# A GATv2 layer on Trainium2: groups of 8 rows with 64 places instead of 32 rows with 16, and one head's relu on ScalarE

## The chip, the cores and the metric

The kernel runs as one program on one core of one Trainium2 chip. The metric is the device time of one execution in microseconds (us). A profiled execution of the same program gives the trace that all views below come from; its span runs from the first to the last instruction of the core. PE is TensorE (PEld its weight loads), DVE is VectorE, ACT is ScalarE, POOL is GpSimd, SP is SyncE.

## What is computed

Two graph layers on 3327 nodes with 128 features, the node count padded to 3328 = 26 blocks of 128. Only layer 0 (four attention heads over a dense adjacency matrix that is about 2% filled) is touched by the change in more than names. Per head:

```python
x1 = x @ w1                       # one row per destination node i
x2 = x @ w2                       # one row per source node j
E = leaky_relu(x1[:, None, :] + x2[None, :, :], 0.01)
s = E @ a
s = exp(tanh(s / 8.0) * 8.0) * A_shape
s = s / sum(s, axis=-1)
out = leaky_relu(s @ x @ Wlin.T, 0.01)
```

The heads are concatenated, multiplied by `w` and added to `x`. Layer 1 is a normalised graph convolution with the same adjacency matrix.

Since leaky_relu(v) = 0.01 v + 0.99 relu(v), the score of an edge (i, j) is 0.01 a.x1_i + 0.01 a.x2_j + 0.99 a.relu(x1_i + x2_j). The kernel also uses relu(x1 + x2) = max(x2, -x1) + x1: with the maximum instead of the relu, the term of x1 outside has to be a.x1 in place of 0.01 a.x1. Both forms occur below.

## The kernel before, in words

All of the work is in `_sparse_layers`. A block is 128 destination rows. Only the filled entries of a row are worked on: each row gets 64 places (32 for each half of the columns), found by DVE with repeated MAX8 and MATCH_REPLACE8 (L422 to L456); entries beyond these are an overflow of two further tiles. A table in DRAM holds, for each node j, a row of adjacency values, features, a term of x2 and the four heads' x2.

**Gathers.** A block is two halves (`hb`) of 64 rows, a half is four windows (`w` 0 to 3) and one overflow window (`w` 4). For a window POOL issues 8 indirect DMAs (L597, tile `g`), one for each tile of 128 edges; for the overflow it issues 2 (tile `ge`). That is 68 a block. There are four `g` buffers. A buffer is free again when the last user of its window, the aggregation (L702), is done; `fetch` then lets the next window's gathers be issued.

**Stage z** (`stage_z`, groups `m` 0 to 8, two to a window; 18 groups a block). A group before the change is 32 rows x 16 places = 4 tiles of 128 edges. For each pair of heads (`hp`) PE turns the gathered x2 of 2 heads x 4 tiles into a PSUM tile `z` of two banks (L624, 8 transposes) and DVE makes `r = max(z, -x1)` of 128x1024 in one instruction (L640). Group 8, the overflow, adds x1 on PE (L629) and takes the maximum of a small part on DVE (L635) and a relu of the rest on ACT (L637).

**Stage r** (`stage_r`) of the group before: PE contracts `r` with `a` for four heads (L653), each head's result in its own 32 rows of the PSUM tile `s`.

**`finish`**, a generator that goes on by one step at each `slot()`, works a window off: ACT copies `s` to `ssb` (L662), DVE makes `wq` (L666), PE turns the scores (L671), DVE adds the terms of x2 and x1 (L674, L677), ACT does tanh and exp (L682, L684), DVE makes the weights `wt` (L693), and PE aggregates (L702): 8 matmuls of 32 output columns, each with an output at partitions 32*cg to 32*cg + 31 and in half `u` of the PSUM tile `ag`. Before the change tile t has cg = t % 4 and u = t // 4, so each window uses all four cg.

**Order.** It is written out by hand, and each engine does its instructions in that order. The main loop emits for group i: a slot, stage z of i (with four slots inside), stage r of i - 1, a slot. A slot advances the finishing generators, a share of the preparation of the next block (`prep`: the adjacency turned by PE and copied by ACT at L365 and L367 with a DMA from ACT's queue at L370, DVE's search for entries, a sum over the whole adjacency rows on ACT at L443, x1 at L553 to L570) and the gathers. Most instructions are emitted some slots before their result is needed.

**Names that the change touches:** `x1n` is -x1 with features on partitions (L561), `pex` the term of x1 outside the relu for each edge (L563 to L570, from `p_all`, whose first four columns are a.x1 and last four 0.01 a.x1), `idx` the row numbers for the gathers, `k.oi` and `x1b` the overflow's selectors.

The line that fixes the PSUM tiles of stage z, two bufs of two banks, is this, used once for heads 0 and 1 and once for heads 2 and 3:

```python
z = ps_z.tile([P, 2, BANK], F32, name="z")
```

Of the kernel before, what the change touches and what calls it, by code (L numbers as in the profile page):

```python
# [9 lines left out]
F32 = mybir.dt.float32  # L10
AF = mybir.ActivationFunctionType
OP = mybir.AluOpType
# [219 lines left out]
def _sparse_layers(tc, nc, x, adj, w1, w2, a, wlin, w, gw, gb, gb_sb, gwT, x_sb, dinv, flag, ident, out):  # L232
# [24 lines left out]
    with ExitStack() as l0:  # L257
# [29 lines left out]
        ph = l0.enter_context(tc.tile_pool(name="ph", bufs=2))  # L287
        pr = l0.enter_context(tc.tile_pool(name="pr", bufs=2))
        pv = l0.enter_context(tc.tile_pool(name="pv", bufs=1))
        pe_ = l0.enter_context(tc.tile_pool(name="pe", bufs=1))  # L290
        ps_tr = l0.enter_context(tc.tile_pool(name="ps_tr", bufs=2, space=PSUM))
        ps_z = l0.enter_context(tc.tile_pool(name="ps_z", bufs=2, space=PSUM))
        ps_s = l0.enter_context(tc.tile_pool(name="ps_s", bufs=1, space=PSUM))
        ps_a = l0.enter_context(tc.tile_pool(name="ps_a", bufs=1, space=PSUM))
        ones = pv.tile([P, D], F32, name="xn")
        nc.vector.memset(ones, 1.0)
# [56 lines left out]
        def prep(b, k):  # L353
# [204 lines left out]
            for h in range(H):  # L558
                nc.tensor.matmul(pm[:, h * P:(h + 1) * P], w1_sb[:, h, :], hTb, start=True, stop=True)
            x1n = pb.tile([P, H, P], F32, name="x1n")  # L560
            nc.scalar.activation(x1n, pm[:, :H * P].rearrange("p (h i) -> p h i", h=H), AF.Copy, scale=-1.0)  # L561
            pmx = pb.tile([P, 16, H], F32, name="pmx")
            nc.vector.tensor_tensor(pmx, tmask[:, :, None].to_broadcast([P, 16, H]),  # L563
                                    p_all[:, b, None, :H].to_broadcast([P, 16, H]), OP.mult)
            yield
# [4 lines left out]
            nc.scalar.copy(pex, pm[:, :16 * H].rearrange("p (t h) -> p t h", h=H))  # L570
            k.x1b, k.x1n, k.pex = x1b, x1n, pex
            yield
# [5 lines left out]
        def gather(b, hb, w):  # L578

            k = blks[b]  # L580
            tab = tables[b % 2].rearrange("(r u) -> r u", u=1)
            if w == NW:
                if b + hb == 0:
                    state["over"] = pe_.tile([P, OVT, WIDE], F32, name="ge")
                    nc.vector.memset(state["over"][HALF:, FOUND:], 0.0)
                g, n, at = state["over"], FOUND, k.idxo[:, hb]
                rows = b * P + HALF * hb
                c0, n0 = (0, FEAT + COLS) if hb == 0 else (FEAT, BODY + FEAT)
                nc.sync.dma_start(g[:HALF, FOUND, :n0], tables[b % 2][:NP * ROW].rearrange("(r c) -> r c", c=ROW)[rows:rows + HALF, c0:c0 + n0])
            else:  # L590
                g, n, at = rows_in(), WT, k.idx[:, w, WT * hb:WT * hb + WT]

            def one(t):
                lo, hi = (0, FEAT + COLS) if hb == 0 else (0, BODY + FEAT)
                if w < NW:
                    lo, hi = (8 * t, hi) if hb == 0 else (0, BODY + 8 * t + 8)
                return nc.gpsimd.indirect_dma_start(out=g[:, t, lo:hi], out_offset=None, in_=tab,  # L597
                                                    in_offset=bass.IndirectOffsetOnAxis(ap=at[:, t:t + 1], axis=0))

            queue.extend((k, hb, w, partial(one, t)) for t in range(n))  # L600
            k.g[hb, w] = g
# [10 lines left out]
        def stage_z(k, hb, m, slot):  # L612
            n = 4 * P if m < 8 else FOUND * P
            arrived(k, hb, m // 2)
            g = k.g[hb, m // 2]
            out = []
            for hp in range(2):
                z = ps_z.tile([P, 2, BANK], F32, name="z")
                r = pr.tile([P, 2, BANK], F32, name=f"r{hp}")
                for i in range(2):  # L620
                    h = 2 * hp + i
                    c0 = k.f0[hb] + PROJ + h * D
                    for q in range(n // P):
                        nc.tensor.matmul(z[:, i, q * P:(q + 1) * P], g[:, m % 2 * 4 + q, c0:c0 + D], ident,  # L624
                                         is_transpose=True, start=(q == 0 or m < 8), stop=(m < 8), skip_group_check=True)
                    if m == 8:
                        nc.tensor.matmul(z[:, i, n:n + HALF], g[:HALF, FOUND, c0:c0 + D], ident[:HALF, :HALF],
                                         is_transpose=True, start=False, stop=False, skip_group_check=True)
                        nc.tensor.matmul(z[:, i, :n], k.x1b[:, h * D:(h + 1) * D], k.oi[:, hb * n:(hb + 1) * n],  # L629
                                         start=False, stop=True, skip_group_check=True)  # L630
                    if i == 0:
                        slot()
                slot()
                if m == 8:
                    nc.vector.tensor_tensor(r[:, :, n:n + HALF], z[:, :, n:n + HALF],  # L635
                                            k.x1n[:, 2 * hp:2 * hp + 2, HALF * hb:HALF * hb + HALF], OP.max)
                    nc.scalar.activation(r[:, :, :n], z[:, :, :n], AF.Relu)  # L637
                else:
                    r0 = HALF * hb + 32 * (m % 2)
                    nc.vector.tensor_tensor(r.rearrange("p h (i s) -> p h i s", s=16), z.rearrange("p h (i s) -> p h i s", s=16),  # L640
                                            k.x1n[:, 2 * hp:2 * hp + 2, r0:r0 + 32, None].to_broadcast([P, 2, 32, 16]), OP.max)
                out.append(r)
            return out

        def stage_r(k, hb, m, rs):
            n = 4 * P if m < 8 else FOUND * P + HALF
            at = m % 2
            if state["scores"] is None:
                state["scores"] = ps_s.tile([P, BANK], F32, name="s")
                nc.vector.memset(state["scores"], 0.0)  # L650
            k.s = state["scores"]
            for h in range(H):
                nc.tensor.matmul(k.s[32 * h:32 * h + 2, :n], sel[:, h, 31 - at:33 - at], rs[h // 2][:, h % 2, :n],  # L653
                                 start=(at == 0), stop=(at == 1 or m == 8))


        def finish(k, hb, w):
# [3 lines left out]
            ssb = ph.tile([P, BANK], F32, name="ssb", bufs=1)  # L661
            nc.scalar.copy(ssb[:, :nk * P], s[:, :nk * P])  # L662
            if w < NW:
                wq = pb.tile([P, WT, 8], F32, name="wq")
                diag = bass.AP(g.tensor, g.offset + BODY * hb, [list(g.ap[0]), [WIDE + 8, 8], [1, 8]])
                nc.vector.tensor_tensor(wq, diag, qmask[:, None, :].to_broadcast([P, WT, 8]), OP.mult)  # L666
            yield
            yield
            pt = ps_tr.tile([P, 4, P], F32, name="tr")
            for q in range(nk):  # L670
# [5 lines left out]
                                    g[:, :, f0 + D:f0 + D + H].rearrange("p (m k) h -> p m k h", m=nm), OP.add)  # L676
            nc.vector.tensor_add(sc[:, :nt], sc[:, :nt], k.pex[:, 8 * hb:8 * hb + 8] if w < NW else  # L677
                                 k.ex[:, OVT * hb:OVT * hb + OVT, 42:42 + H])
            yield
# [11 lines left out]
            if w < NW:  # L691
# [7 lines left out]
                yield  # L699
                for t in range(WT):  # L700
                    u, cg = t // 4, t % 4
                    nc.tensor.matmul(ag[32 * cg:32 * cg + 32, u, :WORK], wt[:, t].rearrange("p h q -> p (h q)"),  # L702
                                     g[:, t, f0:f0 + WORK], start=(w == 0 and t < 4), stop=False, skip_group_check=True)
                allow("g")
# [229 lines left out]
        def strip_in(s):  # L934

            n = min(4, NB - 4 * s)
            r0 = pr.tile([P, 2, BANK], F32, name="r0").rearrange("p k (b d) -> p k b d", b=4)[:, :, :n]
            r1 = pr.tile([P, 2, BANK], F32, name="r1").rearrange("p k (b d) -> p k b d", b=4)[:, :, :n]
            rows = slice(4 * s * P, (4 * s + n) * P)
            nc.sync.dma_start(r0[:, 0], xn_d[rows, :].rearrange("(b p) d -> p b d", p=P))  # L940
            if finished(4 * s):
                nc.sync.dma_start(r1[:, 0], part1_d[:, rows].rearrange("p (b i) -> p b i", b=n))
            if s in early:
                nc.sync.dma_start(r0[:, 1], part2_d[:, rows].rearrange("p (b i) -> p b i", b=n))
            return n, rows, r0, r1

        def strip_out(s, po, n, rows, r0, r1):

            ot, t, xo = r0[:, 1], r1[:, 1], r0[:, 0]
            po = po[:, :n * P].rearrange("p (b i) -> p b i", b=n)  # L950
# [23 lines left out]
        def layer1():  # L974
            ending, sums, ins = [], {}, {}
            for i, (s, j) in enumerate(work):
# [3 lines left out]
                if s not in sums:  # L980
                    sums[s] = ps_z.tile([P, 2, BANK], F32, name="z")[:, 0]
                if j == min(NB - 1, first_column(s) + 4 * (s not in front)):
# [202 lines left out]


        pgs = [l0.enter_context(tc.tile_pool(name=f"pg{i}", bufs=1)) for i in range(4)]

# [167 lines left out]
```

## Time and profile before

| What | Value |
|---|---|
| Time before, median of 12 runs | 2525.42 us (2522.43 to 2528.16) |
| The profiled execution's own time | 2529.1 us |
| Its span | 2527.4 us |
| Granted TensorE clock | 0.98 |
| Instructions | 52430 |
| HBM read and written | 754.47 MB, 113.22 MB |

The page gives a group of instructions as its line, its engine and operation, its operands, a count, the busy time and the mean duration, and behind the second bar the idle time of its engine just before, with what ended it. A timeline line is start, duration, engine, line, operands, count and, in brackets, the idle time before and its releaser. A matmul with four-byte operands is recorded twice unless it is a transpose. The stages that the page shows in 40 slices are: 0 to about 65 us of loading and table building, then the 26 blocks to about 2400 us, then the rest of layer 1. In the blocks the slices hardly differ from each other.

### The profile page before, as it was taken

How to read it: one execution, taken by the hardware profiler on the slowest of the kernel's cores; microseconds unless marked ns; L12 is line 12 of the kernel's file. 1: busy time of each engine (PE TensorE's matmuls, PEld its weight loads, DVE VectorE, ACT ScalarE, POOL GpSimd, SP SyncE). 2: the span in 40 equal slices, each digit the busy share in tenths (PEclk: the TensorE clock that was granted, in tenths of full speed). 3: DMA queues.
4: the chain of work that ended last, by engine and by line, in shares of the span. 5: the costliest groups of instructions: out<-in, count | busy, mean ns of one | idle time of the engine just before them, and what ended most of it. 6: DMA issues, size and time to landing. Idle time of an engine off the chain costs nothing.

```text
span 2527.4 us, 52430 instructions
## 1 busy us (share of the span) xinstructions
PE 2286.5 (90%) x19410; PEld 1579.1 (62%) x19410; DVE 2092.3 (83%) x6478; ACT 687.3 (27%) x1703; POOL 1735.9 (69%) x1822
## 2 busy tenths in 40 slices
PE   6589899989999998999999999999999999999977
PEld 4456666666666666666666666666666666666643
DVE  7688988898898888889889888988988898896623
ACT  4122232223223222322222232222232223222110
POOL 3567777777777776777777777777777777777700
PEclk9799999999999999999999999999999999999999
DMA  9999999999999999999999999999999999999995
GB/s 306 382 321 320 355 330 317 349 347 322 327 356 330 313 346 329 290 337 359 320 323 353 340 315 339 355 318 320 343 339 316 337 349 306 330 325 350 348 273 155
DMA packets 417844, 826.94 MB, mean 327 GB/s; under 512 B 38435, under 2 KB 288815, under 8 KB 414255
## 3 DMA queue, kind: packets, MB, share of 16 engines
q0 software_dynamic: 141440, 619.41, 70.1%
q1 hardware_dynamic: 165343, 147.87, 18.4%
q10 hardware_dynamic: 110800, 56.25, 7.7%
q8 instruction: 156, 2.56, 0.4%
q14 instruction: 105, 0.86, 0.1%
HBM read 754.47 MB, written 113.22 MB: 343 GB/s over the span
## 4 chain that ended last, share of the span: by engine, by line
PE 35%; DVE 28%; DMA 18%; POOL 10%; issue 7%; ACT 0%; SPq 0%; DVEq 0%; ACTq 0%; POOLq 0%
DMA g<-table,idx 14%; DVE r L640 13%; PE z L624 10%; POOL g L597 10%; PE s L653 6%; PE z L629 3%; DVE cand L422 3%; PE ag L702 2%; PE tr L671 2%; DVE cand L456 2%; DVE codes L410 2%; DVE lists L453 2%; DMA g<-AT_d 2%; PE z L985 1%; PE tr L921 1%
## 5 line engine op out<-in xcount | busy, mean ns | idle before, releaser
L597 POOL DMA_INDIRECT g<-table,idx x1664 | 1613.0, 969 | 612.9 <-issue 415.8
L624 PE MATMUL z<-ident,g 128*128 128x128 f32 x6656 | 919.8, 279 | 134.0 <-DVE r L640 115.2
L640 DVE TENSOR_TENSOR r<-z,x1n 128x1024 f32<-128x1024 f32 x832 | 1010.2, 1216 | 35.8 <-PE z L624 34.0
L624 PEld LDWEIGHTS z<-ident,g 128*128 128x128 f32 x6656 | 747.2, 143 | 341.6 <-DVE r L640 226.2
L653 PE MATMUL s<-r,sel 128*2 128x512 f32 (+1 forms) x3744 | 474.5, 579 | 2.8 <-DVE s L650 2.1
L662 ACT COPY ssb<-s 128x512 f32<-128x512 f32 x260 | 146.9, 565 | 476.5 <-PE s L653 469.3
L422 DVE MAX8 cand<-codes 128x8 f32<-128x52 uint16 x1664 | 215.4, 206 | 0.0
L682 ACT ACTIVATE th<-sc 128x32 f32<-128x32 f32 x260 | 58.4, 225 | 464.2 <-DVE sc L677 439.8
L702 PEld LDWEIGHTS ag<-g,wt 128*32 128x32 f32 x3328 | 99.1, 110 | 121.3 <-issue 105.7
L671 PE MATMUL tr<-ident,ssb 128*128 128x128 f32 x988 | 156.7, 279 | 7.6 <-ACT ssb L662 6.3
L367 ACT COPY at<-tr 128x512 f32<-128x512 f32 (+1 forms) x175 | 97.1, 555 | 217.8 <-PE tr L365 200.5
L629 PE MATMUL z<-oi,x1b 128*128 128x256 f32 x416 | 146.4, 434 | 0.0
L453 DVE MAX8 lists<-cand 128x8 f32<-128x272 f32 (+1 forms) x338 | 133.2, 394 | 2.9
L702 PE MATMUL ag<-g,wt 128*32 128x133 f32 x3328 | 134.1, 279 | 1.3 <-DVE wt L693 1.3
L674 DVE TENSOR_TENSOR sc<-tr,g 128x32 f32<-128x32 f32 x208 | 38.5, 185 | 115.3 <-PE tr L671 115.3
L365 PE MATMUL tr<-ident,adjb 128*128 128x128 f32 x676 | 109.8, 286 | 23.4 <-DMA adjb<-in_adj_dram 15.9
L671 PEld LDWEIGHTS tr<-ident,ssb 128*128 128x128 f32 x988 | 111.2, 141 | 27.5 <-ACT ssb L662 19.9
L635 DVE TENSOR_TENSOR r<-z,x1n 128x128 f32<-128x128 f32 x104 | 30.1, 289 | 111.4 <-PE z L629 110.3
L597 POOL DMA_INDIRECT ge<-table,idxo x104 | 99.7, 958 | 31.9 <-issue 13.1
L637 ACT ACTIVATE r<-z 128x512 f32<-128x512 f32 x104 | 62.1, 597 | 215.1 <-DVE r L635 215.1
L456 DVE MATCH_REPLACE8 cand<-lists,cand 128x272 f32<-128x272 f32 (+1 forms) x312 | 118.2, 379 | 0.0
L410 DVE SCALAR_TENSOR_TENSOR codes<-adjb,code 128x832 uint16<-128x832 f32 x104 | 103.2, 1019 | 12.9 <-DMA adjb<-in_adj_dram 12.9
(201 smaller groups left out, 2448.9 us busy)
## 6 DMA issues: line engine op xcount, KB each, us to landing
adjb<-in_adj_dram SPq DMA_DIRECT2D x26, 1664.0 KB
table<-AT_d SPq DMA_DIRECT2D x26, 1664.0 KB
AT_d<-at ACTq DMA_DIRECT2D x150, 256.0 KB
g<-table,idx POOLq DMA_INDIRECT x1664
table<-img SPq DMA_DIRECT2D x12, 1296.0 KB
adjb<-AT_d SPq DMA_DIRECT2D x72, 128.0 KB
g<-AT_d SPq DMA_DIRECT2D x25, 256.0 KB
g<-AT_d ACTq DMA_DIRECT2D x25, 256.0 KB
```

What stands on the lines that cost most here:

```text
L410: nc.vector.scalar_tensor_tensor(codes[:, i], adjb[:, c0:c0 + part], 0.0, code[:, c0:c0 + part], op0=OP.not_equal, op1=OP.mult, accum_out= ...
L422: nc.vector.max(cand[:, c, 8:].rearrange("p (r s) -> p r s", s=32)[:, :, sgm % 32], codes.rearrange("p a b -> p (a b)")[:, sgm % 32 * SEG: ...
L453: nc.vector.max(top, of)
L456: nc.vector.match_replace(out=of, in_to_replace=top, in_values=of, imm_value=0.0)
L597: return nc.gpsimd.indirect_dma_start(out=g[:, t, lo:hi], out_offset=None, in_=tab, in_offset=bass.IndirectOffsetOnAxis(ap=at[:, t:t + 1], ...
L624: nc.tensor.matmul(z[:, i, q * P:(q + 1) * P], g[:, m % 2 * 4 + q, c0:c0 + D], ident, is_transpose=True, start=(q == 0 or m < 8), stop=(m ...
L629: nc.tensor.matmul(z[:, i, :n], k.x1b[:, h * D:(h + 1) * D], k.oi[:, hb * n:(hb + 1) * n], start=False, stop=True, skip_group_check=True)
L640: nc.vector.tensor_tensor(r.rearrange("p h (i s) -> p h i s", s=16), z.rearrange("p h (i s) -> p h i s", s=16), k.x1n[:, 2 * hp:2 * hp + 2 ...
L653: nc.tensor.matmul(k.s[32 * h:32 * h + 2, :n], sel[:, h, 31 - at:33 - at], rs[h // 2][:, h % 2, :n], start=(at == 0), stop=(at == 1 or m = ...
L662: nc.scalar.copy(ssb[:, :nk * P], s[:, :nk * P])
L671: nc.tensor.transpose(pt[:, q, :], ssb[:, q * P:(q + 1) * P], ident)
L702: nc.tensor.matmul(ag[32 * cg:32 * cg + 32, u, :WORK], wt[:, t].rearrange("p h q -> p (h q)"), g[:, t, f0:f0 + WORK], start=(w == 0 and t ...
```

## The change

A group of four tiles is now 8 rows with all 64 places, no longer 32 rows with 16 places. The places of a row come in four chunks of 16, one chunk to a tile, so tile q of a group is chunk q of its 8 rows. A window (8 tiles) is 16 rows with 64 places instead of 64 rows with 16. The 32 tiles of a half are the same tiles; they are gathered in another order. The transposes write their 128 columns as 8 runs of 16 with a stride of 64, so that in a PSUM row the 64 places of a row stand together. ACT's copy of the scores (`ssb`) undoes this.

In groups 0 to 7 the relu of head 0 is done by ACT: eight ACTIVATEs of 128x64, one for each row, with that row's x1 as bias (one value for each partition). DVE does head 1 alone (128x512) and heads 2 and 3 together (128x1024) as before. Heads 0 and 1 each have a PSUM tile of one bank (`za`, `zb`) and a result tile (`ra`, `rb`); heads 2 and 3 share `zc` and `rc`. These PSUM tiles have one buffer each; `z` had two of two banks. The total is four banks in both. For head 0 `pex` uses 0.01 a.x1, since ACT's form is the relu. A new tile `x1p` holds +x1 of head 0 (one ACT copy of 128x128 a block).

In the overflow group heads 0 and 1 get an instruction each on DVE and on ACT where they shared one. In the aggregation a window now uses two of the four cg instead of all four, each for four tiles, taken in turn.

The core of the diff:

```diff
-        pr = l0.enter_context(tc.tile_pool(name="pr", bufs=2))
-        ps_z = l0.enter_context(tc.tile_pool(name="ps_z", bufs=2, space=PSUM))
+        prs = l0.enter_context(tc.tile_pool(name="prs", bufs=2))
+        zs = l0.enter_context(tc.tile_pool(name="zs", bufs=1, space=PSUM))
...
             x1n = pb.tile([P, H, P], F32, name="x1n")
             nc.scalar.activation(x1n, pm[:, :H * P].rearrange("p (h i) -> p h i", h=H), AF.Copy, scale=-1.0)
+            x1p = pb.tile([P, P], F32, name="x1p")
+            nc.scalar.copy(x1p, pm[:, :P])
-            nc.vector.tensor_tensor(pmx, tmask[:, :, None].to_broadcast([P, 16, H]),
-                                    p_all[:, b, None, :H].to_broadcast([P, 16, H]), OP.mult)
+            for h0, h1, of in ((0, 1, H), (1, H, 0)):
+                nc.vector.tensor_tensor(pmx[:, :, h0:h1], tmask[:, :, None].to_broadcast([P, 16, h1 - h0]),
+                                        p_all[:, b, None, of + h0:of + h1].to_broadcast([P, 16, h1 - h0]), OP.mult)
...
+            t0 = WT * hb + 2 * w
             def one(t):
+                own = 8 * (2 * w + t // 4)
+                which = at[:, t % 4, t0 + t // 4:t0 + t // 4 + 1] if w < NW else at[:, t:t + 1]
                 if w < NW:
-                    lo, hi = (8 * t, hi) if hb == 0 else (0, BODY + 8 * t + 8)
+                    lo, hi = (own, hi) if hb == 0 else (0, BODY + own + 8)
...
+            r0 = HALF * hb + 8 * m
             for hp in range(2):
-                z = ps_z.tile([P, 2, BANK], F32, name="z")
-                r = pr.tile([P, 2, BANK], F32, name=f"r{hp}")
+                if hp:
+                    zc, rc = zs.tile([P, 2, BANK], F32, name="zc"), prs.tile([P, 2, BANK], F32, name="rc")
+                    zz, rr = [zc[:, i] for i in range(2)], [rc[:, i] for i in range(2)]
+                else:
+                    zz = [zs.tile([P, BANK], F32, name=name) for name in ("za", "zb")]
+                    rr = [prs.tile([P, BANK], F32, name=name) for name in ("ra", "rb")]
...
-                        nc.tensor.matmul(z[:, i, q * P:(q + 1) * P], g[:, m % 2 * 4 + q, c0:c0 + D], ident,
+                        to = zz[i][:, q * P:(q + 1) * P] if m == 8 else zz[i].rearrange("p (i q s) -> p q i s", q=4, s=16)[:, q]
+                        nc.tensor.matmul(to, g[:, m % 2 * 4 + q, c0:c0 + D], ident,
...
+                    elif h == 0:
+                        for e in range(8):
+                            at = slice(e * HALF, (e + 1) * HALF)
+                            nc.scalar.activation(rr[0][:, at], zz[0][:, at], AF.Relu, bias=k.x1p[:, r0 + e:r0 + e + 1], scale=1.0)
+                    elif h == 1:
+                        nc.vector.tensor_tensor(rr[1].rearrange("p (i s) -> p i s", s=HALF), zz[1].rearrange("p (i s) -> p i s", s=HALF),
+                                                k.x1n[:, 1, r0:r0 + 8, None].to_broadcast([P, 8, HALF]), OP.max)
...
-                    nc.vector.tensor_tensor(r.rearrange("p h (i s) -> p h i s", s=16), z.rearrange("p h (i s) -> p h i s", s=16),
-                                            k.x1n[:, 2 * hp:2 * hp + 2, r0:r0 + 32, None].to_broadcast([P, 2, 32, 16]), OP.max)
+                elif hp:
+                    nc.vector.tensor_tensor(rc.rearrange("p h (i s) -> p h i s", s=HALF), zc.rearrange("p h (i s) -> p h i s", s=HALF),
+                                            k.x1n[:, 2:, r0:r0 + 8, None].to_broadcast([P, 2, 8, HALF]), OP.max)
...
-            nc.scalar.copy(ssb[:, :nk * P], s[:, :nk * P])
+            if w < NW:
+                nc.scalar.copy(ssb.rearrange("p (q i s) -> p q i s", q=4, s=16), s.rearrange("p (i q s) -> p q i s", q=4, s=16))
...
-                for t in range(WT):
-                    u, cg = t // 4, t % 4
-                    nc.tensor.matmul(ag[32 * cg:32 * cg + 32, u, :WORK], wt[:, t].rearrange("p h q -> p (h q)"),
-                                     g[:, t, f0:f0 + WORK], start=(w == 0 and t < 4), stop=False, skip_group_check=True)
+                for q in range(4):
+                    for m in range(2):
+                        t, u, cg = 4 * m + q, (2 * w + m) // 4, (2 * w + m) % 4
+                        nc.tensor.matmul(ag[32 * cg:32 * cg + 32, u, :WORK], wt[:, t].rearrange("p h q -> p (h q)"),
+                                         g[:, t, f0:f0 + WORK], start=(w < 2 and q == 0), stop=False, skip_group_check=True)
```

`wq` and the addition of `pex` follow the new order of tiles with instructions of the same size. The pools of the first stage (`pr`, `ps_z`) are closed before the main loop, and layer 1 uses `za`, `zb`, `ra`, `rb` and `rc` where it used `z`, `r0` and `r1`.

## The prediction

> **What bounds the kernel now.** I read the page's engine line first. PE, DVE and POOL are all high, so shares don't decide.
>
> ```profile
> PE 2286.5 (90%) x19410; PEld 1579.1 (62%) x19410; DVE 2092.3 (83%) x6478; ACT 687.3 (27%) x1703; POOL 1735.9 (69%) x1822
> ```
>
> Next the timeline of POOL where one block's gathers end and the next one's begin, here at two such places.
>
> ```profile
> 1157.02 1.10 POOL L597 DMA_INDIRECT ge<-table,idxo  x1 [0.30 <-PE tr L743]
> 1160.06 0.95 POOL L597 DMA_INDIRECT g<-table,idx  x1 [1.94 <-PE ag L702]
> ...
> 1248.44 0.94 POOL L597 DMA_INDIRECT g<-table,idx  x1 [1.94 <-PE ag L702]
> ```
>
> Two things are to be seen. A block takes 1248.44 - 1160.06 = 88.4 us. And POOL issues a gather every 0.95 + 0.30 = 1.25 us; 68 of them are 85.3 us, so POOL is nearly full. But once a block it waits 1.94 us for a `g` buffer, and what frees that is PE's aggregation. So the chain PE-DVE sets the pace (in the waits PE hardly ever stops for a gather: 9.7 us in all for `PEld z`), and POOL forms a floor: no more than 88.4 - 85.3 = 3.1 us a block can be had.
>
> Who holds up PE is in the view of the line L640, under "who waited for it":
>
> ```profile
>   PEld z L624: 253.7, 245
>   PE z L624: 117.3, 152
> ```
>
> It is DVE's maximum. Where, the table of busy times over one block shows, cut by me where the character changes (columns: stretch, us, then PE, PEld, DVE, ACT, POOL busy, clock, DMA share, GB/s):
>
> ```profile
> 1071.70:1083.50 11.80, 10.06 (x95) 6.31 (x93) 11.56 (x35) 4.22 (x7) 8.80 (x10) 1.00 1.03 390
> 1083.50:1096.40 12.90, 12.89 (x108) 8.74 (x112) 11.08 (x29) 3.14 (x8) 9.77 (x10) 1.00 1.04 391
> 1096.40:1108.40 12.00, 9.95 (x95) 7.12 (x88) 11.69 (x29) 2.07 (x8) 9.17 (x10) 1.00 1.04 357
> 1108.40:1137.30 28.90, 28.34 (x252) 19.74 (x253) 21.59 (x65) 8.77 (x26) 21.89 (x24) 1.00 0.88 287
> 1137.30:1160.10 22.80, 20.66 (x195) 15.56 (x193) 22.45 (x90) 7.24 (x18) 15.98 (x18) 1.00 1.01 324
> ```
>
> Rows 1, 3 and 5 (46.6 us) are **DVE stretches**: DVE works 45.7 us, PE idles 1.74 + 2.05 + 2.14 = 5.9. Rows 2 and 4 (41.8 us) are **PE stretches**: PE idles 0.6 and DVE has 9 us to spare. What is saved on DVE counts in the first, what is added on PE counts in the second.
>
> **The change part by part.** *DVE.* L640 takes 1216 ns for 128x1024. For 128x512 with one operand in PSUM, L962 takes 690. So a group costs 690 + 1216 in place of 2432: 0.53 us less. A block has 16 such groups: 8.4 us. The overflow's split is two of about 219 (L666, 128x64) for one of 289 (L635), 0.15 us twice a block, and `pmx` in two adds about 0.17; the three fall into PE stretches. Of the 16 groups, about 10 have their stage z in DVE stretches (by PE's timeline: 3, 3 and 4): 5.3 us less there, DVE comes to 40.4.
>
> *ACT.* Eight ACTIVATEs of 128x64 with a bias for each partition. The nearest row is at the start, four of 128x128 with such a bias:
>
> ```profile
> 6.90 1.28 ACT L1055 ACTIVATE cen<-x_sb,neg 128x128 f32<-128x128 f32 x4 [0.67 <-DVE neg L1046]
> ```
>
> One is 384 to 402 ns (mean 389), so they follow each other by (1.28 - 0.39) / 3 = 0.30. ACT's copies of 128 and 512 columns (266 and 586 ns) give 0.83 ns a column, so 64 columns fewer are 0.053 less: 0.25 each, 8 x 0.25 + 0.1 = 2.1 us a group. Bounds: eight of the bare 128x64 copy L570 (212 ns, overlapping by 0.09) are 1.1; eight of 389 with no overlap 3.1. I take 2.1, since L1055 has the same operands. In the DVE stretches ACT then has 13.5 + 10 x 2.1 = 34.5 us, and 2.6 us of DMA issue on its queue (seven of 0.37 at L370): 37 of 46.6. It fits. Where it is tightest is row 5: 7.2 + 2.2 + 4 x 2.1 = 17.8 of 22.8. For the whole block ACT goes from 25 to about 60 of 88. `x1p` is one copy of 266 ns a block, in row 4, where ACT is idle for 20 us; without that cover 0.3 us a block.
>
> The Trainium skill speaks against this move: "ScalarE: Activation LUTs", section "Rules for kernel authors", gives relu and max to VectorE. The durations here agree on the cost, 2.1 us on ACT for 0.53 of DVE. By the rule alone this is a loss of 1.6 us of engine time a group; by the table above DVE is full where it counts and ACT isn't, so I don't charge the difference.
>
> *The added waits.* PE's za of the next group now waits for ACT's eight relus, where it waited for DVE. On ACT, behind a waiting relu stand `ssb`, tanh/exp and the copies of the turned adjacency; PE's L671 and L365 and DVE's `wt` wait for those. From za's end to the next za PE has zb, zc, the scores and some other work, over 3.5 us, against 2.1 us; so ACT may be late by about 1.5 us without cost. The worst case is L443, 2.98 us once a block at the end of row 5 (1159.86 in ACT's timeline). It stands behind one group's relus and ahead of the next one's, and by my count (2.1 + 2.98 + 0.46 for tanh and exp + 2.1) those end 7.6 us after the first za, before PE, at 4.3 us a group, needs the tile for the group after the next. Lower bound nothing; upper bound that all of L443 is a wait: 3 us a block.
>
> *PE.* The transposes stay the same in number and size. No row shows a matmul that writes with a stride; I take no cost, as the columns written are as many, and leave a loss out of the range. But the aggregation changes:
>
> ```profile
> 1149.66 1.72 PE L721 MATMUL ag<-ge,wo 128*128 128x133 f32 x12
> ...
> 1159.12 0.64 PE L702 MATMUL ag<-g,wt 128*32 128x133 f32 x16
> ```
>
> Both stream 133 columns. L721 has outputs on all 128 partitions and goes one at a time: less about 0.28 for the last one's latency (277 ns at L702), 1.44 / 12 = 0.12 each. L702 does 16 in 0.64, that is four at once (0.28 + 3 rounds of 0.12): its outputs lie in four different groups of 32 partitions. After the change a window has only two such groups. Bounds: as now, or one at a time, 0.28 + 15 x 0.12 = 2.08. I take two at once, 8 rounds: 0.28 + 7 x 0.12 = 1.12, as each group of partitions gets 8 of the 16. That is **+0.48 us a window**, 8 windows a block, 3.8 us. By PE's timeline five of the eight lie in PE stretches (1088.68, 1096.39, 1111.04, 1121.69, 1132.77): +2.4 us there, in full on the path. Three lie in DVE stretches: +1.4, inside PE's idle time.
>
> *Gathers.* Same tiles, same bytes (widths 653 to 712, each four times a half), same 68 instructions, other order: nothing.
>
> *Sum for a block.* DVE stretches: PE's floor is 46.6 - 5.9 + 1.4 = 42.1, DVE's 40.4, ACT's 37. Two engines within 2 us of each other that wait for each other in turn don't reach the floor; between 42.1 (-4.5) and 46.6 (0) I take 43.2, **-3.4**. PE stretches: **+2.4**. Net -1.0 us, over the 25 blocks after the first: -25 us. Start and tail stay. Made against the profiled execution's own 2529.1 this is 2504; the median of the runs lies 3.7 us below that execution: **2500 us**. POOL's wait of 1.94 us a block should then shrink to about 1; that is the next thing that is late.
>
> **The rivals.** (1) *Full relief.* PE reaches its floor in the DVE stretches: -4.5 + 2.4 = -2.1 a block, -53 us, 2473; POOL's floor (-3.1) is near. For it: PE's busy time counts the latency of matmuls before each idle gap, so its real floor is lower. Against it: the many in-order waits. (2) *Nothing left.* The DVE stretches give back just the 2.4 us: 2525, within 0.2%. (3) *Slower: PE waits for ACT where it waited for DVE.* The DVE stretches keep their 46.6 us because the single za isn't handed back in time, and the PE stretches pay 2.4: +60 us, 2585. It decides when relus and the other work of ACT between two za of a group exceed the group's 4.3 us; in row 5 two adjacency copies with their DMA issues (2 x 0.96), `ssb` (0.59) and the relus (2.1) are 4.6, so it is close, and POOL's wait would then grow to about 4 us. A half of it, +30 us, is as likely as the whole. (4) *The aggregation goes one at a time*: 8 x 1.44 = 11.5 more on PE a block, less the 3.4: about +8, 203 us in all, 2728.
>
> **How the numbers follow.** Forecast 0.44, full relief 0.06, nothing left 0.13, ACT on the path 0.30, one at a time or slower writes 0.07. So faster by over 0.2% (about what a measurement of this kernel can tell from no change) 0.50, within 0.2% 0.13, slower 0.37. The range goes from 2468, just under full relief, to 2580, most of the third rival; beyond it are the rest of that rival and the fourth.
>
> **What would show it.** Right: `rb` at about 0.69 us x416, PE's waits for DVE under half of the 371 us now, the L702 group at about 1.1 us a window, PE's waits for ACT's `ra` under 40 us in all, POOL's wait at the block's start near 1 us. Wrong: relus far from 2.1 us a group; transposes no longer 0.11 us apart; `PE za` waiting for ACT for a microsecond in many groups; or aggregation still in 0.64 us, which alone would be worth 2.4 us a block, so far as POOL's floor lets it through.

## The result, and the profile after

| What | Value |
|---|---|
| Time after, median of 7 runs | 2558.95 us (2554.08 to 2564.54) |
| The kernel before beside it, median of 28 runs | 2524.83 us (2520.37 to 2531.83) |
| Ratio, 95% interval | 1.0133 [1.0122, 1.0144] |
| The profiled execution's own time, its span | 2553.83 us, 2552.0 us |
| Granted TensorE clock | 0.978 |

The change made the kernel 1.3% slower, some 34 us. The forecast was 25 us faster.

The engine line of the page after:

```profile
PE 2393.1 (94%) x19410; PEld 1664.7 (65%) x19410; DVE 1878.6 (74%) x6556; ACT 1390.6 (54%) x5109; POOL 1756.6 (69%) x1822
```

DVE was relieved of 214 us (2092 to 1879) and ACT took 703 us more (687 to 1391), as meant. PE, which does the same number of matmuls, is busy 107 us longer. The groups that the change made or altered:

```profile
L651 ACT ACTIVATE ra<-za,x1p 128x64 f32<-128x64 f32 x3328 | 727.9, 330 | 299.3 <-PE za L638 276.3
L663 DVE TENSOR_TENSOR rc<-zc,x1n 128x1024 f32<-128x1024 f32 x416 | 504.8, 1213 | 15.4 <-PE zc L638 14.8
L653 DVE TENSOR_TENSOR rb<-zb,x1n 128x512 f32<-128x512 f32 x416 | 285.1, 685 | 276.4 <-PE zb L638 270.9
...
L734 PE MATMUL ag<-g,wt 128*32 128x133 f32 x3328 | 226.5, 279 | 0.0
```

The aggregation (L734) was busy 134.1 us before and is 226.5 now: +92 of PE's +107. Note also the end of the `rb` row: DVE now sits idle for 270.9 us until PE has made `zb`. DVE now waits for PE far longer than PE for DVE. PE's side of that, from the waits (total, times, longest):

```profile
PEld za L638 <- ACT ra L651: 54.6, 68, 5.5
PEld zc L638 <- DVE rc L663: 49.6, 89, 2.1
...
PEld tr L380 <- ACT at L368: 37.8, 36, 1.2
...
PE zc L638 <- DVE rc L663: 28.4, 63, 1.7
...
PE tr L380 <- ACT at L368: 19.2, 20, 1.0
```

The waits for DVE's maximum fell from 371 to 78 us. Others stand in their place, and the two largest of these end with ACT: the relu `ra`, and `at`, ACT's copy of the turned adjacency. L380 (L379 before) is where PE multiplies that copy with rows of layer 1 that are already finished, so there is more of it the later the block: 2 matmuls a block at first, 22 in block 23 (4 and 44 records; blocks are counted from 0). Idle time ahead of this line isn't new: PE and its weight loads together stood 69.5 us there before (13.8 of them until `at`, the rest until DVE's `sc` or for nothing that the profile shows) and stand 60.7 now, 57.0 of them until `at`.

**The loss isn't spread evenly.** Two blocks, an early one and a late one, each from its first gather to the next block's, by busy time (columns as in the prediction's table). The kernel before:

```profile
532.30:620.50 88.20, 81.41 (x719) 56.86 (x718) 78.25 (x242) 26.33 (x67) 66.64 (x68) 0.98 0.98 334
1870.40:1959.60 89.20, 83.61 (x752) 59.53 (x751) 79.17 (x246) 25.61 (x65) 65.59 (x69) 1.00 0.98 336
```

The changed kernel:

```profile
533.10:620.30 87.20, 84.06 (x723) 59.50 (x722) 69.65 (x244) 52.47 (x197) 66.50 (x68) 1.00 0.98 339
1866.20:1956.90 90.70, 87.99 (x752) 62.77 (x750) 70.68 (x249) 52.72 (x195) 67.25 (x68) 1.00 0.96 326
```

Before, PE had 6.8 and 5.6 us idle in these blocks. After, it has 3.1 and 2.7, so nearly all of the block is PE's. The early block got 1.0 us shorter, the gain forecast for every block; the late one got 1.5 us longer. That the early one meets the forecast is in part luck: POOL issues the 68 gathers of this block without a pause of over 0.31 us between two, and still needs 87.2 us for them, as several take longer than 0.95 (up to 1.79). The forecast had 85.3 for that. By the first gathers of all blocks in POOL's timeline, blocks 2 to 12 take 13 us less in all, blocks 13 to 23 take 16 us more. Some 6 of the 13 us stand in one long block of the execution before (95.5 us from 976.0 on). In the two kernels with the strips moved (below) the same sums are 973.3 and 969.6 for blocks 2 to 12, 981.3 and 993.6 for 13 to 23, so the early gain is small and the late loss holds. The last two blocks up to the last gather take 5 more, what comes after the last gather 15 more (126.9 to 142.0), the start 2 more: the 24.6 us by which the two spans differ.

POOL's wait at a block's start, which the prediction also named, in POOL's timeline of the changed kernel, in a middle block and a late one:

```profile
1148.74 0.95 POOL L605 DMA_INDIRECT g<-table,idx  x1 [0.87 <-PE za L638]
```

```profile
2139.83 0.95 POOL L605 DMA_INDIRECT g<-table,idx  x1 [4.69 <-PE za L638]
```

It is 0.87 us where 1.94 was near by, and 4.69 late in the run, where the same block before had 3.62 (at 2138.30): PE holds the `g` buffers longer.

### The profile page after: what moved, and what is told of

The parts are those of the page before. It is cut to its first block, busy times and chain, and to the rows that moved or that the text cites. A ratio compares the mean times of both kernels' runs of the same rounds, so it can differ in the third digit from the quotient of the medians.

```text
span 2552.0 us, 55879 instructions
## 1 busy us (share of the span) xinstructions
PE 2393.1 (94%) x19410; PEld 1664.7 (65%) x19410; DVE 1878.6 (74%) x6556; ACT 1390.6 (54%) x5109; POOL 1756.6 (69%) x1822
## 4 chain that ended last, share of the span: by engine, by line
PE 67%; DVE 10%; ACT 10%; DMA 9%; issue 2%; POOL 1%; SPq 0%; ACTq 0%; DVEq 0%; POOLq 0%
PE s L676 13%; PE zc L638 10%; PE za L638 7%; PE ag L734 6%; ACT ra L651 6%; PE zb L638 4%; DMA g<-table,idx 4%; PE tr L698 4%; DVE rc L663 3%; PE zc L643 3%; PE ag L753 3%; PE tr L380 2%; DVE codes L411 2%; DVE rb L653 2%; ACT adjb L444 2%
## 5 line engine op out<-in xcount | busy, mean ns | idle before, releaser
L651 ACT ACTIVATE ra<-za,x1p 128x64 f32<-128x64 f32 x3328 | 727.9, 330 | 299.3 <-PE za L638 276.3
L663 DVE TENSOR_TENSOR rc<-zc,x1n 128x1024 f32<-128x1024 f32 x416 | 504.8, 1213 | 15.4 <-PE zc L638 14.8
L653 DVE TENSOR_TENSOR rb<-zb,x1n 128x512 f32<-128x512 f32 x416 | 285.1, 685 | 276.4 <-PE zb L638 270.9
L638 PE MATMUL zc<-ident,g 128*128 128x128 f32 x3328 | 452.0, 277 | 33.2 <-DVE rc L663 28.4
L676 PE MATMUL s<-rc,sel 128*2 128x512 f32 x1872 | 469.1, 579 | 0.0
L676 PE MATMUL s<-ra,sel 128*2 128x512 f32 x936 | 466.1, 580 | 2.6 <-DVE s L673 1.9
L676 PE MATMUL s<-rb,sel 128*2 128x512 f32 x936 | 466.0, 580 | 0.0
L638 PEld LDWEIGHTS zc<-ident,g 128*128 128x128 f32 x3328 | 378.1, 142 | 66.2 <-DVE rc L663 49.6
L638 PE MATMUL za<-ident,g 128*128 128x128 f32 x1664 | 272.1, 285 | 13.4 <-DMA g<-table,idx 6.8
L734 PEld LDWEIGHTS ag<-g,wt 128*32 128x32 f32 x3328 | 187.0, 110 | 125.9 <-issue 72.9
L638 PE MATMUL zb<-ident,g 128*128 128x128 f32 x1664 | 252.5, 275 | 0.0
L734 PE MATMUL ag<-g,wt 128*32 128x133 f32 x3328 | 226.5, 279 | 0.0
```

The source lines that it names most:

```text
L638: nc.tensor.matmul(to, g[:, m % 2 * 4 + q, c0:c0 + D], ident, is_transpose=True, start=(q == 0 or m < 8), stop=(m < 8), skip_group_check=True)
L651: nc.scalar.activation(rr[0][:, at], zz[0][:, at], AF.Relu, bias=k.x1p[:, r0 + e:r0 + e + 1], scale=1.0)
L653: nc.vector.tensor_tensor(rr[1].rearrange("p (i s) -> p i s", s=HALF), zz[1].rearrange("p (i s) -> p i s", s=HALF), k.x1n[:, 1, r0:r0 + 8, ...
L663: nc.vector.tensor_tensor(rc.rearrange("p h (i s) -> p h i s", s=HALF), zc.rearrange("p h (i s) -> p h i s", s=HALF), k.x1n[:, 2:, r0:r0 + ...
```

## The experiments

Three theories were set against each other. **Theory 1:** PE is now the bound, and the aggregation's +92 us fill what the relief freed. **Theory 2:** PE waits for ACT, where it waited for DVE. **Theory 3:** the loss sits at the end, where ACT stands at layer 1's strip DMAs with relus queued behind. Below, a time in us that follows from a difference of ratios is that difference x 2525.

**Eight first runs, not used.** Four kernels, twice each, ran on a chip where the kernel before took 3385 us (first four) and 3311 us (second four), so that no conclusion for 2525 us can be drawn from them. Their edits are shown below, where they ran again. What was expected, and what came:

Aggregation in four column groups: 3594.84 us, 1.0604 [1.0551, 1.0657], and 3498.49 us, 1.0547 [1.0488, 1.0605].

> The changed kernel with one thing put back: in the aggregation tile t goes to cg = t % 4 and u = t // 4 as before the change, so four groups of partitions are in use in every window; the sums of tiles of different rows are mixed by this, so it leaves out the right assignment of sums to rows. Theory 1 (PE has become the bound, chiefly by the aggregation, whose busy time rose from 134 to 226 us): that busy time goes back to 134, PE falls by about 90 us, POOL's floor stops the gain before all of it comes through, 2490 to 2520 us. Theory 2 (PE waits for ACT's eight relus of head 0, the third rival of the prediction): 2550 to 2562 us, as the changed kernel.

> The edit of e1_ag4 again (the changed kernel with tile t at cg = t % 4, u = t // 4 in the aggregation, sums of tiles of different rows mixed), beside a kernel before that takes its usual 2525 us. Theory 1 (PE is the bound, by the aggregation): its busy time back from 226 to 134 us, 2490 to 2520 us. Theory 2 (PE waits for ACT's relus): 2550 to 2562 us.

The kernel before with two column groups: 3435.98 us, 1.0152 [1.0108, 1.0197], and 3363.07 us, 1.0155 [1.0118, 1.0191].

> The kernel before with the new aggregation order alone: two groups of partitions in a window (sums of tiles of different rows mixed, as in e1). Theory 1: +3.8 us of PE a block, of which 2.4 to 3.8 come through, 2585 to 2620 us. Theory 2: the aggregation is not the cause, 2525 to 2540 us.

> The edit of e2_before_ag2 again (the kernel before with the new aggregation order alone, sums mixed), beside a kernel before at its usual 2525 us. Theory 1: 2585 to 2620 us. Theory 2: 2525 to 2540 us.

Head 0's relu on DVE: 3549.53 us, 1.0472 [1.0423, 1.052], and 3389.22 us, 1.0237 [1.0166, 1.0308].

> The changed kernel with head 0's maximum on DVE (one 128x512 with -x1, like head 1), so that ACT has none of the new work; everything else stays. Theory 1: the aggregation's cost stays and DVE is full again, 2590 to 2630 us. Theory 2: without ACT's relus on the path the time goes back to 2525 to 2545 us.

> The edit of e3_h0_dve again (the changed kernel with head 0's maximum on DVE), beside a kernel before at its usual 2525 us. Theory 1: 2590 to 2630 us. Theory 2: 2525 to 2545 us.

Strips on SP: 3659.13 us, 1.0822 [1.0774, 1.087], and 3569.55 us, 1.0779 [1.0736, 1.0822]. On that chip the four come out in another order than below; why isn't known.

> The changed kernel, but all DMAs that bring layer 1's strips of the adjacency are issued by SP; before, every second one was on ACT's queue. Theory 3 (of the loss in the profile, about 15 us lie behind the last gather, where ACT stands at a strip's DMA and the relus behind it hold up PE): 10 to 15 us less than the changed kernel, 2543 to 2550 us. If the end of the run has another cause: 2556 to 2562 us.

> The edit of e4_strips_sp again (the changed kernel with all DMAs of layer 1's strips issued by SP), beside a kernel before at its usual 2525 us. Theory 3 (ACT stands at a strip's DMA near the end and the relus behind it hold up PE): 2543 to 2550 us. Another cause of the longer end: 2556 to 2562 us.

**The changed kernel again**, as a base.

> The changed kernel itself, unaltered, beside the kernel before, as the base for the ratios of the others. All theories: 2545 to 2565, some 1.3% above the kernel before.

Measured: 2554.34 us, 1.0134 [1.0104, 1.0165]. The difference from the kernel before is the one of the result.

**Aggregation in four column groups.** The changed kernel with the order of before in `finish`; its sums land in other rows, so the output isn't the layer's.

```diff
-                for q in range(4):
-                    for m in range(2):
-                        t, u, cg = 4 * m + q, (2 * w + m) // 4, (2 * w + m) % 4
+                for t in range(WT):
+                    u, cg = t // 4, t % 4
...
```

> The changed kernel (2554 here) with its aggregation's 16 matmuls a window spread over four column groups again instead of two; the sums are then added to the wrong rows, so the output is not the reference's, and no instruction is added or left out. Theory 1 (the changed kernel is bound by PE, and the aggregation's extra 92 us fill it): 2490 to 2520, faster than before. Theory 2 (PE waits for ACT's relus): 2545 to 2560, since PE only waits longer. Theory 3 (the loss sits in the last block, where ACT stands at its strip DMAs): a gain of at most 10, 2544 to 2554.

Measured: 2503.4 us, 0.9923 [0.9901, 0.9945], that is 53 us less than the changed kernel. Theory 1 holds here, and the other two miss. The same two blocks:

```profile
526.70:612.90 86.20, 80.23 (x717) 55.56 (x717) 69.01 (x241) 52.09 (x196) 65.48 (x69) 1.00 0.99 343
1832.00:1919.80 87.80, 84.64 (x753) 59.56 (x752) 70.56 (x249) 52.73 (x196) 66.13 (x69) 1.00 0.98 338
```

The late block is 2.9 us shorter than the changed kernel's, with PE 3.4 us less busy. The early one is at 86.2 us, and POOL has no pause of over 0.31 us between its gathers; in blocks 2 to 12 POOL's waits beyond these 0.30 us are 0.15 us a block. So the aggregation's saving can't count in full in early blocks.

**The slower aggregation alone**, in the kernel before (the same edit the other way round; the sums land in other rows).

> The kernel before (2523 here) with its aggregation's 16 matmuls a window in two column groups at a time, as in the changed kernel; the sums are added to the wrong rows, and no instruction is added or left out. Theory 1 (this alone costs the changed kernel its gain): 2575 to 2600, near the changed kernel with the relus back on DVE (2586). Theory 2 (it is hidden in DVE's waits, and ACT's relus cost the time): 2525 to 2540.

Measured: 2578.87 us, 1.0227 [1.021, 1.0245]: +57 us. Two kernels give the same price, so it is the aggregation's own.

**Head 0's relu back on DVE**, in the changed kernel.

```diff
-                        for e in range(8):
-                            at = slice(e * HALF, (e + 1) * HALF)
-                            nc.scalar.activation(rr[0][:, at], zz[0][:, at], AF.Relu, bias=k.x1p[:, r0 + e:r0 + e + 1], scale=1.0)
+                        nc.vector.tensor_tensor(rr[0].rearrange("p (i s) -> p i s", s=HALF), zz[0].rearrange("p (i s) -> p i s", s=HALF),
+                                                k.x1n[:, 0, r0:r0 + 8, None].to_broadcast([P, 8, HALF]), OP.max)
```

(`pmx` takes the columns of a.x1 for all heads again.)

> The changed kernel with head 0's relu on DVE again (one max over heads 0 and 1 in 1.2 us, then head 2's), its aggregation in two column groups kept; the output is unchanged. Theory 1: both costs at once, 2590 to 2630. Theory 2: without ACT's relus the wait for ACT goes, and the time returns toward before, 2525 to 2545. Theory 3: 2535 to 2550 if the last block alone is relieved and DVE's extra time is hidden.

The expectation has one thing wrong: as `za` and `zb` are separate tiles, DVE does two maxima of 0.68 us (the trace has L649 and L652, 416 each), not one of 1.2. Measured: 2586.11 us, 1.0239 [1.0213, 1.0265]: 27 us more than the changed kernel. So moving head 0 to ACT does gain in this layout, even with what it costs on ACT. Two maxima take some 0.15 us more than one for both heads, but against the kernel before with the slower aggregation, which has one, the changed kernel is 24 us shorter as well. Theories 2 and 3 are wrong here, and theory 1's figure is a little high.

**The strips on SP's queue**, in the changed kernel.

```diff
-                eng = nc.scalar if k % 2 else nc.sync
+                eng = nc.sync
```

> The changed kernel with layer 1's strip DMAs all issued on SP's queue instead of on SP's and ACT's in turn, so that ACT's relus of the last block do not stand behind them; the output is unchanged. Theory 3: 10 to 15 us faster, 2540 to 2546. Theories 1 and 2: 2550 to 2558; slower than 2560 if SP's queue becomes the bound at the end.

Measured: 2537.22 us, 1.0053 [1.0036, 1.007]: 20 us less. In the changed kernel the chain that ended last has, ahead of stage z in the last block:

```profile
2409.98 8.29 DMA adjb<-AT_d
2418.27 0.02 issue
2418.29 4.40 DMA g<-AT_d
2422.69 0.04 issue
2422.73 1.76 ACT ra L651 x8
2424.49 0.04 issue
2424.53 1.12 PE za L638 x4
```

PE's transposes at 2424.53 wait for eight relus, and these for a strip's DMA (`g<-AT_d`). ACT's own waits after 2300 us have the same:

```profile
ACT ra L651 <- DMA g<-AT_d: 14.8, 2, 8.3
```

A relu doesn't read a strip; it stands behind the DMA of the next one in ACT's order. With the strips on SP that wait is gone, and what follows the last gather takes 122.2 us in place of 142.0. Theory 3 is right about a part, and the gain is above its 10 to 15.

**The same edit in the kernel before.**

> The kernel before with layer 1's strip DMAs on SP's queue alone; the output is unchanged. Theory 3 (the strips cost the changed kernel time because relus stand behind them on ACT's queue, and the kernel before has no such relus): 2518 to 2530, no change beyond a few us. If the strips on ACT's queue cost both kernels alike, it is not the change's cost: 2505 to 2512.

Measured: 2514.58 us, 0.9968 [0.9955, 0.9981]: 8 us less, between the two ranges. The strips cost the kernel before as well; there tanh (`th`) stands 24.2 us behind them in three waits. So of the 20 us, about 12 come with the change. This version, with its output unchanged, is the fastest of those that compute the layer.

**Both together**, aggregation in four groups (sums in other rows) and strips on SP.

> The changed kernel with both: aggregation in four column groups (sums added to the wrong rows) and layer 1's strip DMAs on SP's queue alone. If the two costs are separate, as theories 1 and 3 together have it, their gains add (51 and 17 below 2554): 2480 to 2492. If they are one and the same time counted twice: 2500 to 2506.

Measured: 2480.8 us, 0.9828 [0.9812, 0.9845]: 77 us less than the changed kernel, and 53 + 20 = 73. The two costs are separate.

**One short relu**, in the changed kernel; the term x1 of head 0 is left out, so that ACT has one instruction of 128x512 a group.

```diff
-                        for e in range(8):
-                            at = slice(e * HALF, (e + 1) * HALF)
-                            nc.scalar.activation(rr[0][:, at], zz[0][:, at], AF.Relu, bias=k.x1p[:, r0 + e:r0 + e + 1], scale=1.0)
+                        nc.scalar.activation(rr[0], zz[0], AF.Relu)
```

> The changed kernel with one ACT relu of 128x512 for head 0 in place of eight of 128x64 (x1 of head 0 is left out of the sum), so ACT has about 1.2 us a group less, some 490 us in all, and PE and DVE have the same work as in the changed kernel. Theory 1 (PE with the slower aggregation is the bound): 2540 to 2556, at most the waits for ACT's relus (62 us in the changed kernel's trace) come back in part. Theory 2 (PE waits for ACT): 2495 to 2520. Theory 3: a few us of the last block, within theory 1's range.

Measured: 2513.54 us, 0.9951 [0.9928, 0.9973]: 46 us less. This is theory 2's range, and theory 1 alone is out. By the spans, 28 of the 41 us between the profiled executions are won in blocks 13 to 23, 11.5 after the last gather, none in blocks 2 to 12. There was little to be won in the early ones: POOL's waits beyond its 0.30 us between gathers are 5.9 us in blocks 2 to 12 of the changed kernel and 32.6 in blocks 13 to 23. Where the late ones win, the view of the line L380 shows under "its engine sat idle before it (us, times) until". The changed kernel:

```profile
L380 PE MATMUL tr<-at,x_sb x488: 275/275/377, 336.7 to 2229.0; 128*128 128x128 f32 x163
...
  ACT at L368: 57.0, 56
```

With the one short relu:

```profile
L380 PE MATMUL tr<-at,x_sb x488: 275/275/377, 332.3 to 2201.1; 128*128 128x128 f32 x163
...
  ACT at L368: 16.7, 24
```

And one such place in a late block, PE's timeline and then ACT's, of the changed kernel:

```profile
1938.77 0.60 PE L366 MATMUL tr<-ident,adjb 128*128 128x128 f32 x4
...
1941.25 1.16 PE L380 MATMUL tr<-at,x_sb 128*128 128x128 f32 x8 [1.00 <-ACT at L368]
```

```profile
1938.97 1.75 ACT L651 ACTIVATE ra<-za,x1p 128x64 f32<-128x64 f32 x8 [2.81 <-PE za L638]
1940.56 0.64 ACT L368 COPY at<-tr 128x512 f32<-128x512 f32 x1
```

PE has turned the adjacency at 1939.37, but the copy stands behind the relus, which end at 1940.72, and starts at 1940.56 (ACT's instructions overlap a little); PE's next matmuls (L380) need the copy and stand for 1.00 us. With one short relu the same pair reads:

```profile
1921.94 0.60 ACT L649 ACTIVATE ra<-za 128x512 f32<-128x512 f32 x1 [2.82 <-PE za L638]
1922.43 0.58 ACT L368 COPY at<-tr 128x512 f32<-128x512 f32 x1
```

There L380 starts at 1923.07 with no idle time.

The totals alone don't say which wait counts: until `ra` PE and its weight loads stand 62.1 us ahead of stage z in the changed kernel and 9.7 with the short relu, a larger fall than that of L380. But most of this is idle time of the weight loads, while matmuls still run. PE's own waits for ACT in blocks 13 to 23 of the changed kernel (1237.4 to 2232.2) are these two alone:

```profile
PE tr L380 <- ACT at L368: 14.4, 15, 1.0
...
PE tr L366 <- ACT at L368: 2.6, 9, 0.5
```

With the short relu 0.5 us of these 17.0 are left. So in the late blocks PE's matmuls stand not for the relus' result but for the copy queued behind them. That is 16.5 of the 28 us won there. In all PE idles 18 us less and is busy 10 us less; where these 10 belong the trace doesn't say, and no run puts the copy ahead of the relus.

**Groups of 16 rows by 32 places**, an attempt at a better version. A window then has four groups of eight rows, so the aggregation uses four column groups, with its output unchanged; head 0 needs 16 ACTIVATEs of 128x32, and the strips are on SP.

```diff
-                        for e in range(8):
-                            at = slice(e * HALF, (e + 1) * HALF)
+                        for e in range(16):
+                            at = slice(e * 32, (e + 1) * 32)
...
-                        t, u, cg = 4 * m + q, (2 * w + m) // 4, (2 * w + m) % 4
+                        t, u = 4 * (cg // 2) + 2 * c + cg % 2, w // 2
```

> A version of the change with groups of 16 rows by 32 places, so that a window holds four groups of eight rows and its aggregation uses four column groups; head 0's relu on ACT in 16 instructions of 128x32 instead of 8 of 128x64; strips on SP's queue; one more small DVE instruction a window; the output is unchanged. Theories 1 and 3: 2485 to 2505, if ACT's 16 (an estimate of 3.1 us a group from the spacing of the eight, 220 ns) stay beside PE's work. If ACT becomes the wait (theory 2): above 2530.

Measured: 2711.28 us, 1.0735 [1.0711, 1.076]. A miss. The sixteen take 2.95 us, and now PE does wait for the relus themselves (its matmuls 101.7 us, its weight loads 199.2):

```profile
PEld za L637 <- ACT ra L650: 199.2, 140, 2.6
...
PEld tr L380 <- ACT at L368: 93.9, 54, 2.7
```

**The same with ACT in every second group only**, DVE taking two maxima of 0.69 in the others.

```diff
-                    elif h == 0:
+                    elif h == 0 and m % 2 == 0:
...
-                    elif h == 1:
+                    elif h < 2:
```

(`pmx` takes the column of head 0 by the group it belongs to.)

> Groups of 16 rows by 32 places as in e8 (aggregation in four column groups, strips on SP's queue), but head 0's relu on ACT only in every second group; in the others DVE takes heads 0 and 1 in two maxima of 0.69 us; the output is unchanged. Per pair of groups DVE has 1906 + 2596 = 4502 ns in place of 4864, 2.9 us a block less; ACT has half of e8's relus, 24 us a block. If e8 was slow because ACT stood full (69% and in order), 2490 to 2510, below the kernel before with its strips moved (2515); if the 16 short relus of a group are late by themselves, 2540 to 2650.

Measured: 2612.03 us, 1.0348 [1.0327, 1.037]. ACT is busy 49% here, less than in the changed kernel, and PE still waits 169 us for `ra` and 91 for `at` at L380. So how full ACT is doesn't decide alone. That the length of the row of relus does, fits this run and the one short relu. It isn't shown by itself, as this version also has another order of places and more work on DVE (2019 us busy, 1879 in the changed kernel).

## Why the prediction was wrong, point by point

- **What bounds the kernel.** Right for before. That POOL is a floor was confirmed: with four column groups the early blocks came down to 86.2 us and POOL hardly waited any more. The floor was put too low: blocks in which POOL doesn't wait at all take 86.0 to 87.4 us, not 85.3, so early blocks had less to gain than the 3.1 us.
- **DVE.** Durations right: 685 and 1213 ns, 8.5 us a block. The gain was taken as 3.4 us a block in the DVE stretches, -85 us. From head 0 on DVE (1.0239) to one short relu on ACT (0.9951) is 0.0288, -73 us: about right, where the relu on ACT is short.
- **PE's aggregation.** Right. 1.12 us a window was predicted:

```profile
1872.17 1.10 PE L734 MATMUL ag<-g,wt 128*32 128x133 f32 x16
```

  Its price, +60 us (2.4 a block), came out at 57 in the kernel before and 53 in the changed one. Less the 0.28 us of the last matmul, the sixteen records (8 matmuls, each recorded twice) take 0.36 us with four groups in use and 0.82 with two. The Trainium skill, "TensorEngine Tiling (Array Packing)", section "Theoretical Speedup", gives up to four times where the small dimension is 32 or less; the row with four groups agrees.
- **ACT. This step failed.** The eight relus take 1.76 us (2.1 predicted), ACT is as busy as was worked out (52 to 53 us a block of about 60), and it was taken to cost nothing: "ACT may be late by about 1.5 us without cost". The price was +46 us. The step named the copies of the turned adjacency as standing behind the relus, but it measured their lateness against the next `za` alone, 3.5 us on. L380 needs `at` much sooner (in the pair shown PE is free for it at 1940.25, 1.3 us after the end of `za`), and the step didn't list it. Of the 41 us between the two spans, 28 lie in blocks 13 to 23, where PE's own idle time until `at` is 17.0 us with eight relus and 0.5 with one. It also worked from one block in the middle of the run, at 1071 us; L380's share grows to the end, and the late blocks lost more than the early ones won. The engine's share of a stretch (37 of 46.6 us) said that ACT's work fits, but not when each result is due.
- **"Start and tail stay." This failed too**, by 15 us after the last gather. Relus were put on a queue that also issues the strips' DMAs; the move past that queue wasn't counted. Some 12 us of the strips' 20 are the change's. (The 46 us of the ACT step hold part of these: of the relus' 41 us in the spans, 11.5 lie after the last gather.)
- **The sum.** The ratios split the change into +60 (head 0 on DVE in the new layout, 1.0239), -73 (its relu on ACT, were it short) and +46 (eight relus for the short one). These are differences from one run to the next, so they must add up to the change's own +34 (33 with rounding) and are no check of it. Predicted: +60, -85 and 0. So the sign was lost at the ACT step.
- **The rivals.** The third, "PE waits for ACT where it waited for DVE", came closest, with its half price of +30. Its mechanism was only partly what happened: it looked for the wait at `za`, where the trace has 62 us, 54.6 of them the weight loads' and 7.4 PE's own, in two waits. At L380 it has 57, 19.2 of them PE's own in 20 waits. The rival's condition (ACT's work between two `za`) leaves L380 out. The fourth is ruled out by 1.10 us a window. Which part of the 62 us at `za` is due to the relus themselves and which to things queued ahead of them, these runs don't separate.
- **What would show it.** `rb`, the waits for DVE, the aggregation's 1.10 and the transposes' spacing came as forecast. "PE's waits for ACT's `ra` under 40 us" did not (62), nor did POOL's wait outside the middle blocks.

Not tried: ACT's copy of the turned adjacency placed ahead of the relus in ACT's order, which the L380 view suggests.

## What to carry to other kernels

When work is moved to an engine with time to spare, list every instruction queued behind it and when its reader needs it; the reader that is due first can set the price, where the engine's share shows nothing. Check this in an early and in a late part of the run, and in the tail, where the queue may hold DMA issues. And when a layout changes the order of small matmuls, count how many groups of output partitions each burst still uses.

## What the runs showed of the hardware that wasn't expected

The group of the eight relus (in the changed kernel) and that of the sixteen (groups of 16 rows) have nearly the same median duration, though one has twice the columns (duration in ns: least, median, longest):

```profile
L651 ACT ACTIVATE ra<-za,x1p x3328: 294/330/374, 80.5 to 2439.1; 128x64 f32<-128x64 f32 x196
L650 ACT ACTIVATE ra<-za,x1p x6656: 267/335/416, 80.0 to 2608.6; 128x32 f32<-128x32 f32 x196
```

The median misleads: in both traces the recorded time grows along a row of instructions that follow each other without a pause, from 314 to 357 ns in the eight and from 287 to 396 in the sixteen (medians of the first and the last). The first of a row, which starts on an idle ACT, shows the width: 27 ns less for 32 columns less, 0.84 ns a column, near the 0.83 that the prediction took from ACT's copies. Starts are 0.197 us apart in the eight and 0.170 in the sixteen, so half the columns save 0.027 us each, and 2 x 32 columns cost far more than 64: 2.95 us a row against 1.76.

The Trainium skill, "ScalarE: Activation LUTs", section "What ACT_TABLE_LOAD costs", gives 280 + 0.833 ns a column for an ACTIVATE with such a bias, and 93 ns of overlap back to back. An estimate from these figures is 333 and 307 ns, with starts 240 and 214 ns apart. The cost of a column agrees; the first of a row is some 20 ns shorter here, and the starts some 43 ns closer.
